# A two-layer graph network on one Trainium2 core: the first pair's transpose moved to TensorE, and the closing work of the last pairs and the planner's VectorE room rearranged

## The chip, the cores and the metric

The kernel runs on one core of a Trainium2 chip. The metric is the device time of one execution in microseconds. Before the change the median of three runs is 1908.55 us (1906.41 to 1909.11); the profiled execution has a span of 1906.8 us. The engines are TensorE (PE in the profile; its weight loads, PEld, are counted apart), VectorE (DVE), ScalarE (ACT), GpSimd (POOL) and SyncE (SP), which issues the transfers. All arithmetic is in float32.

## What is computed

There are 64 graphs of 256 nodes with 512 features, an adjacency of 256 x 256 for each, and two layers. The mask is all ones here.

```python
# layer 0
deg = sum(adj, -1)
agg = (adj @ x) / max(deg, 1e-6)
x   = layernorm(x + relu(concat([x, agg]) @ W.T))
# layer 1
q, k = split(x @ Wqk);  v = x @ Wv
agg  = adj @ (k * mask)
w    = mask * sum(q * agg, -1) / sqrt(512)
x    = layernorm(x + softmax(w, over nodes)[:, :, None] * v)
```

## The kernel before

**Tiling.** Graphs are worked in 32 pairs (`NP`); `k` is the graph of the pair, `t` one of two blocks of 128 nodes, `F` is 512 and `HF` is 256. The products with the weights are done by a Strassen-Winograd scheme of seven products instead of eight, twice nested in part: sums and differences of the blocks of one operand are built first. For the transposed features these are called `xT_s`, `xT_i` (first layer) and `x1T_s`, `x1T_i` (second layer), for the adjacency `sa`, for the aggregated value `tv` (four of them, T1 to T4, made by `sums_T`, line 387). A matrix product with 256 output columns takes two TensorE records, and so does one with 512.

**What a pair goes through.** Layer 0: products with `W` into `own` and `y`; then `gather` (line 401) multiplies the adjacency with `y` and its `tv`, adds parts to `own` and leaves the rest in `z` (this is z's aggregation); `norm0` (line 521) adds `z`, the relu and the residual and normalises `own`, which is then x1. x1 must be transposed for layer 1: `turn` lets VectorE transpose blocks of 32 x 32, and `place` sends the tile `turn` by 16 transfers of 64 KB to `x1T`. Layer 1: products with the weights into `q` (in the tile `y`) and `v`, a second `gather` into `agg`, scores by `dot`. The scores go through DRAM to a row (`send_scores`, `fetch_scores`); `softmax` (line 583) takes the exponentials, `finish` (line 601) adds the weighted `v` to x1 (the steps "adds"), normalises (the steps "finish": `less` on VectorE, two squares and the factor on ScalarE, `shift` on VectorE, two scales on ScalarE) and sends the result out. In the last pair there is no later pair to hide behind, so its x1 is transposed by TensorE (`turn_last`, line 619), into PSUM banks from which ScalarE copies.

**The loop.** Each turn `j` of the loop (line 751) runs layer 0 of pair `j` with layer 1 of pair `j - 1` and the softmax and closing norm of pair `j - 2`. The tail behind the loop (from line 898) does layer 1 of the last pair, the softmax and closing norm of the pair next to last, and then those of the last.

**What sets the order.** Every instruction keeps its place in the program, so the order on each engine is the order of the source's calls. TensorE's order is written out by hand in strings: `run("s s j s a b j", ...)` pops one unit of work from each named list. For the parts that matter here: `r` is the last inner product of layer 0 (which completes `y`), `s` the products whose result goes to the second half of `own`, `a` to `g` are the seven parts of the aggregation (a and b read `y`; c, d, e need `tv` T1, T2, T3; d, e and g write the same PSUM bank as a, so each must wait until the earlier value was read), `j` and `k` are the units of layer 1's first two inner products, `h`, `n`, `q`, `p`, `l` its others.

**The planner.** VectorE's and ScalarE's work that isn't tied to a matrix product stands in chains. A chain has a rank, a name and steps, each for one engine. After each unit `tick` (line 150) takes the first step, in order of rank, whose engine is planned to be free within `room` (0.6 us) of the clock that `mm` advances, and whose `ready` time has come; `step` (line 142) sets this time after a change of engine: 1.4 us after a VectorE step, 2.2 in the closing norms, 0.4 after a ScalarE step. `quiet` stops this, `flush` places all remaining steps of the named chains at once. If VectorE's `tv` are to be spread, `gather` places them one at a time by `spare()`.

Of the kernel before, what the change touches and what calls it, by code (L numbers as in the profile page):

```python
# [94 lines left out]
def resnorm_kernel(  # L95
# [15 lines left out]
    NT, NF, NA = N // P, F // P, A // P  # L111
    H, HF = NF // 2, F // 2
    NP = B // 2
# [16 lines left out]
    clock, chains, shared, quiet = [0.0], [], [1.0], [False]  # L130
    vec = InOrder(tc, nc.vector, clock, lambda name, n: shared[0] * ((0.17 if name == "bn_stats" else 0.07) + n / 960))
    act = InOrder(tc, nc.scalar, clock,
                  lambda name, n: 0.07 + n / 1200 if name == "copy" else (0.3 if n == F else 0.2) + n / 1000)
    gp = InOrder(tc, nc.gpsimd, clock, lambda name, n: 0.0)
    room = {vec: 0.6, act: 0.6}

    def queue(rank, name, *steps, ready=0.0):

        chains.append((rank, name, [ready], deque(steps)))
        chains.sort(key=lambda c: c[0])  # L140

    def step(chain):
        _, name, ready, steps = chain
        eng, work = steps.popleft()
        work()
        ready[0] = eng.free + (2.2 if name == "finish" and eng is vec else 1.4 if eng is vec else 0.4) if steps and steps[0][0] is not eng else 0.0
        if not steps:
            chains.remove(chain)

# [9 lines left out]
    def flush(*names):  # L159
        while True:  # L160
            c = next((c for c in chains if not names or c[1] in names), None)
            if not c:
                return
            step(c)

    def run(order, **units):
        for name in order.split():
            units[name].pop(0)()
# [124 lines left out]
    def inner_sums(X, eng, part):  # L293

        if X.s is None:
            X.open_sums()
        of_sum = lambda n: lambda k, e: X.s[:, k, X.slot[n]:X.slot[n] + 1, e]
        ks, b = ((slice(0, 2), X.first_row), (slice(2, 3), of_sum(S1)), (slice(0, 1), of_sum(S4)))[part]
        a11, a12, a21, a22 = (b(k, e) for k in range(2) for e in range(2))
        i = [X.i[:, r, ks] for r in range(4)]  # L300
        for to, op, c, d in ((i[0], OP.add, a21, a22), (i[1], OP.subtract, i[0], a11),
                             (i[2], OP.subtract, a11, a21), (i[3], OP.subtract, a12, i[1])):
            eng.tensor_tensor(to, c, d, op=op)
# [217 lines left out]
    def norm0(j):  # L521

        own, z, rdeg = owns[j], zs.pop(j), rdegs.pop(j)
        x1Ts[j] = Side(pool, "x1T", S2)
        sq = []

        def scaled(k, t):
            o = own[:, k, t, HF:]  # L530
            vec.scalar_tensor_tensor(o, z[:, k, t], rdeg[:, k, t:t + 1], o, op0=OP.mult, op1=OP.add)

        def residual(k, t, total):
            o = own[:, k, t]
            vec.scalar_tensor_tensor(o, o, 0.0, xs[j][:, k, t], op0=OP.max, op1=OP.add,
                                     accum_out=total[:, t:t + 1])

        def turn(k, t):
            if not sq:
                sq.append(pool.tile([P, 2 * NT * F], F32, name="turn").rearrange(  # L540
                    "p (b k c t q) -> p b k c t q", b=P // Q, k=2, c=NF, t=NT))
            vec.transpose(sq[0][:, :, k, :, t].rearrange("p b c q -> p c b q"), own[:, k, t])

        def place(r):
            to = x1Ts[j].a.rearrange("f k h e t (a q) -> f (k h e t) a q", q=Q)
            for n in r:
                a, b = n // (P // Q), n % (P // Q)
                send(to[b * Q:(b + 1) * Q, :, a],
                     sq[0][a * Q:(a + 1) * Q, b].rearrange("p k c t q -> p (k c t) q"))
        places[0] = place  # L550
        for k in range(2):
            total = small.tile([P, NT], F32, name="sum")
            work = []
            for t in range(NT):
                work += [(vec, lambda k=k, t=t: scaled(k, t)),
                         (vec, lambda k=k, t=t, total=total: residual(k, t, total))]
            steps = work + norm_of(own[:, k], total)
            if j < NP - 1:
                def last(k=k, scale=steps[-1][1]):
                    scale()  # L560
                    queue(1.5, "norm", *[(vec, lambda k=k, t=t: turn(k, t)) for t in range(NT)], ready=act.free + 0.4)
                steps[-1] = (act, last)
            queue(1, "norm", *steps)
# [37 lines left out]
    def finish(j):  # L601

        v, x1 = vs[j], owns.pop(j)

        sums = [small.tile([P, NT], F32, name="sum") for _ in range(2)]

        def add(k, t):
            vec.scalar_tensor_tensor(x1[:, k, t], v[k][:, t], probs[j][:, k, t:t + 1], x1[:, k, t],
                                     op0=OP.mult, op1=OP.add, accum_out=sums[k][:, t:t + 1])

        def last(k, scale):
            scale()
            first(out[2 * j + k].rearrange("(t p) f -> p t f", p=P), x1[:, k])
        queue(0, "adds", *[(vec, lambda k=k, t=t: add(k, t)) for k in range(2) for t in range(NT)])
        for k in range(2):
            steps = norm_of(x1[:, k], sums[k])
            queue(3, "finish", *steps[:-1], (act, lambda k=k, scale=steps[-1][1]: last(k, scale)))

    def turn_last(X, x1, k, ps):
        for t in range(NT):  # L620
            for c in range(NF):
                tc.keep_in_program_order(nc.tensor.matmul(
                    ps[t][:, c * P:(c + 1) * P], x1[:, k, t, c * P:(c + 1) * P], ident, is_transpose=True,
                    start=(c == 0), stop=True, skip_group_check=True))
            act.copy(X.a[:, k, :, :, t].rearrange("p h e m -> p (h e) m"), ps[t].rearrange("p (c m) -> p c m", c=NF))
# [125 lines left out]
    for j in range(NP):  # L751
        X = Xs.pop(j)
# [49 lines left out]
        flush("w0")  # L802
        run("r q r m", m=m, q=q, r=r)
        if j == 1:
            flush("norm")
            places[0](range(16))
            flush("mask")
            sumsM[0] = adj_sums(0)
            load_rows(2)
        quiet[0] = j < 2  # L810
        run("r s r", r=r, s=s)
        if j > 0:
            Y = x1Ts.pop(j - 1)
            inner_sums(Y, gp, 0)
            sums_Y = (*outer_sums(Y, vec), (vec, lambda: inner_sums(Y, gp, 1)))
        if j > 1:
            queue(1, "sums", *sums_Y)
        T_late = []
        T = sums_T(ys[j], T_late)

        if j == 0:
            degrees(1)
# [11 lines left out]
        if j == 0:  # L834
            sums_next()
            held = [c for c in chains if c[1] == "w1"]
            chains[:] = [c for c in chains if c[1] != "w1"]
            early.append(inner("P1", Xs[1], W0, pw[0], u, lambda fifth: early[1](fifth)))
            run("s s a b s d c e i g f", s=s, i=early[0], **g)
            quiet[0] = False  # L840
        else:
            u2, o2, y2 = o, pf, y
            b1, b2, b3, b4, b5, b6, b7, b8 = layer1(j - 1, ys[j][:, :, 0], o2, u2, y2)
            jj = inner("P1", Y, W1, pw[0], u2)
            k = inner("P2", Y, W1, y[0], o2, b2)
            if j == 1:
                run("s s a b s d c e g f", s=s, **g)
                quiet[0] = False
                flush("w1")
                queue(1, "sums", *sums_Y)  # L850
                run("j k j k j k j", j=jj, k=k)
                b1(None)
                run("k", k=k)
            else:
                run("s s j s a b j", s=s, j=jj, k=k, **g)
                if j < NP - 1:
                    degrees(j + 1)
                run("c d j k e j", s=s, j=jj, k=k, **g)
                quiet[0] = True
                run("k", k=k)  # L860
                quiet[0] = False
                b1(None)
                run("g f", **g)
# [34 lines left out]
    send_scores(j - 1)  # L898
    run("l", l=open1)
    flush("norm", "mask")  # L900
    turn_last(X, x1, 0, pf)
    T = sums_T(x1)
    fetch_scores(j - 1)
    sumsM[j] = adj_sums(j)
    turn_last(X, x1, 1, pw)
    inner_sums(X, gp, 0)
    u, o, y = pf, pu, py
    aggs[j] = late.tile([P, 2 * N_SIDE], F32, name="agg").rearrange("p (k t f) -> p k t f", k=2, t=NT)
# [14 lines left out]
    inner_sums(X, gp, 1)  # L923
    run("c d i m e i m", i=i, m=m, **g)
    softmax(j - 1)
    run("g i f i", i=i, **g)
    v = pool.tile([P, 2, NT, F], F32, name="x")
    vs[j] = [v[:, k] for k in range(2)]
    run("m n h h m n h h", h=h, m=m, n=n)
    fourth_sums(X)  # L930
    run("n q q q q n", q=q, n=n)
    flush("softmax", "adds")
    closing = [c for c in chains if c[1] == "finish"]
    for n in (1, 3):
        for c in closing:
            for _ in range(n):
                step(c)
    quiet[0] = True
    run("p p p", p=p)
    for c in closing:  # L940
        step(c)
    run("r p r", p=p, r=r)
    w = small.tile([P, 2, NT], F32, name="w", bufs=1)
    scale_scores(j, w)
    last = [softmax_last(k, w, pu[k]) for k in range(2)]
# [55 lines left out]
```

## Time and profile before

| view | what it shows |
|---|---|
| page, busy times | TensorE 1870.5 us of 1906.8, VectorE 1531.5, ScalarE 1296.3, GpSimd 902.1 |
| windows of 58 us in the middle of the run | TensorE busy 57.6 to 57.9, clock 1.00 |
| window 0 to 100 us | TensorE busy 89.27, mean clock 0.97 |
| window 1856 to 1906 us | TensorE busy 32.48 of 50, mean clock 0.83 |
| groups, VectorE | `turn<-own` x124, 686 ns each; `tv<-y` x64, 721 ns; `x1T_s<-x1T` x64, 693 ns |
| groups, TensorE | transposes at L622 x16, 272 ns a record |
| transfers | `x1T<-turn` x496 of 64 KB, 2.3 us to landing |

The page gives shares over the whole span. The windows say where these shares are not kept: the loop's turns are all alike, the first 100 us and the tail differ. The records of matrix products overlap, so the time that one takes is read from the start of one to the start of the next, not from its length. A bracket at the end of a timeline line gives the idle time of that engine just before it, and what ended it. The helpers at lines 90, 173 and 178 issue nearly everything, so instructions are told apart by the tiles they write and read (`out<-in`).

### The profile page before, as it was taken

How to read it: one execution, taken by the hardware profiler on the slowest of the kernel's cores; microseconds unless marked ns; L12 is line 12 of the kernel's file. 1: busy time of each engine (PE TensorE's matmuls, PEld its weight loads, DVE VectorE, ACT ScalarE, POOL GpSimd, SP SyncE). 2: the span in 40 equal slices, each digit the busy share in tenths (PEclk: the TensorE clock that was granted, in tenths of full speed). 3: DMA queues.
4: the chain of work that ended last, by engine and by line, in shares of the span. 5: the costliest groups of instructions: out<-in, count | busy, mean ns of one | idle time of the engine just before them, and what ended most of it. 6: DMA issues, size and time to landing. Idle time of an engine off the chain costs nothing.

```text
span 1906.8 us, 24867 instructions
## 1 busy us (share of the span) xinstructions
PE 1870.5 (98%) x6980; PEld 1313.5 (69%) x6980; DVE 1531.5 (80%) x3186; ACT 1296.3 (68%) x3266; POOL 902.1 (47%) x1187
## 2 busy tenths in 40 slices
PE   9899999999999999999999999999999999999996
PEld 5567777667677667677677676677776776776774
DVE  7777888878887878887888887888788788878786
ACT  3467776677767677767677766677776777676765
POOL 4455443545444544534554435554445454445431
PEclk9999999999999999999999999999999999999998
DMA  6323334333333433343433343333343333334211
GB/s 222 78 48 96 102 95 112 89 84 98 101 102 94 106 80 99 89 117 84 106 85 98 94 117 84 92 92 106 95 109 91 84 98 98 105 94 107 78 56 45
DMA packets 389160, 182.30 MB, mean 96 GB/s; under 512 B 272160, under 2 KB 353696, under 8 KB 389024
## 3 DMA queue, kind: packets, MB, share of 16 engines
q1 hardware_dynamic: 389024, 180.72, 35.6%
q8 instruction: 57, 0.93, 0.2%
q14 instruction: 79, 0.65, 0.1%
HBM read 114.10 MB, written 34.06 MB: 78 GB/s over the span
## 4 chain that ended last, share of the span: by engine, by line
PE 75%; DVE 12%; SPq 6%; DMA 3%; issue 2%; ACT 1%; POOL 0%; DVEq 0%; POOLq 0%; ACTq 0%
PE bank L173 75%; SPq L178 6%; DVE own L90 4%; DVE y L90 2%; DMA x<-x 2%; DVE x1T_s L90 2%; DVE v L90 1%; DMA x1T<-turn 1%; DVE tv L90 1%; DVE turn L90 1%; ACT y L90 1%; DVE less L90 1%; ACT junk L90 0%; ACT own L90 0%; DVE x L90 0%
## 5 line engine op out<-in xcount | busy, mean ns | idle before, releaser
L90 ACT COPY bank<-bank 128x256 f32<-128x256 f32 (+1 forms) x768 | 332.9, 436 | 196.5 <-PE bank L173 191.0
L90 DVE TENSOR_TENSOR y<-bank,y 128x512 f32<-128x512 f32 x256 | 170.3, 685 | 141.4 <-ACT y L90 137.8
L90 POOL TENSOR_TENSOR x1T_s<-x1T,x1T_s 128x512 f32<-128x512 f32 x32 | 53.1, 1658 | 383.0 <-PE bank L173 383.0
L90 ACT ACTIVATE junk<-own,less 128x512 bf16<-128x512 f32 x252 | 181.6, 721 | 70.3 <-DVE less L90 68.3
L173 PE MATMUL bank<-tv,sa 128*128 128x256 f32 x768 | 199.1, 383 | 5.9 <-DVE tv L90 5.2
L90 ACT ACTIVATE own<-own,shift,rstd 128x512 f32<-128x512 f32 x255 | 197.4, 811 | 0.0
L173 PEld LDWEIGHTS bank<-tv,sa 128*128 128x128 f32 x768 | 142.9, 190 | 64.2 <-issue 22.9
L90 ACT COPY y<-bank 128x512 f32<-128x512 f32 x192 | 108.9, 585 | 96.2 <-PE bank L173 93.4
L90 POOL TENSOR_TENSOR sa<-adj 128x256 f32<-128x256 f32 x128 | 95.5, 746 | 160.9 <-DMA adj<-adj_t 152.2
L173 PE MATMUL bank<-w,x1T_s 128*128 128x512 f32 (+1 forms) x384 | 168.8, 522 | 0.0
L90 POOL TENSOR_TENSOR x1T_i<-x1T 128x256 f32<-128x256 f32 x64 | 57.9, 905 | 234.1 <-DMA x1T<-turn 221.4
L173 PE MATMUL bank<-t_i,x1T_i 128*128 128x256 f32 x512 | 154.1, 384 | 9.8 <-POOL x1T_i L90 5.1
L173 PE MATMUL bank<-t,xT_s 128*128 128x512 f32 (+1 forms) x384 | 159.9, 525 | 0.8 <-ACT own L90 0.3
L173 PE MATMUL bank<-t,x1T_s 128*128 128x512 f32 (+1 forms) x384 | 158.1, 521 | 0.3 <-ACT y L90 0.3
L90 DVE TENSOR_TENSOR v<-bank,v 128x512 f32<-128x512 f32 x186 | 119.1, 681 | 48.9 <-PE bank L173 48.9
L173 PE MATMUL bank<-w,xT_s 128*128 128x512 f32 (+1 forms) x384 | 153.1, 521 | 0.0
L173 PE MATMUL bank<-t_i,xT_i 128*128 128x256 f32 x512 | 152.6, 380 | 0.4 <-DVE own L90 0.2
L173 PEld LDWEIGHTS bank<-t_i,x1T_i 128*128 128x128 f32 x512 | 98.0, 192 | 77.8 <-issue 53.6
L90 ACT COPY own<-bank 128x512 f32<-128x512 f32 x128 | 71.5, 584 | 115.0 <-PE bank L173 74.2
L173 PEld LDWEIGHTS bank<-t_i,xT_i 128*128 128x128 f32 x512 | 94.7, 189 | 58.4 <-issue 46.9
L173 PE MATMUL bank<-t,x1T 128*128 128x512 f32 x256 | 130.4, 592 | 0.0
L90 POOL TENSOR_TENSOR x1T_i<-x1T_s 128x128 f32<-128x128 f32 x128 | 90.2, 705 | 76.3 <-DVE x1T_s L90 73.8
(156 smaller groups left out, 4597.5 us busy)
## 6 DMA issues: line engine op xcount, KB each, us to landing
x<-x SPq DMA_DIRECT2D x64, 512.0 KB, 5.7
xT<-x_t SPq DMA_DIRECT2D x62, 512.0 KB, 5.6
x1T<-turn SPq DMA_DIRECT2D x496, 64.0 KB, 2.3
out<-own SPq DMA_DIRECT2D x62, 512.0 KB, 3.3
adj<-adj_t SPq DMA_DIRECT2D x64, 256.0 KB, 3.8
turn<-adj SPq DMA_DIRECT2D x64, 256.0 KB, 3.0
row<-d SPq DMA_DIRECT2D x31, 256.0 KB, 4.8
wqk<-wqk_t SPq DMA_DIRECT2D x4, 512.0 KB, 5.4
```

The lines of the kernel that those rows point to most:

```text
L90: return self.tc.keep_in_program_order(getattr(self.engine, name)(out, *args, **kwargs))
L173: tc.keep_in_program_order(nc.tensor.matmul(ps, a, b, start=start, stop=True, skip_group_check=True))
L178: return tc.keep_in_program_order(nc.sync.dma_start(out, in_))
```

## The change

It has four edits.

1. **The first pair's x1** is no longer transposed by VectorE and transfers. `turn_last` is now called `turn_here` and is used in the turn `j == 1` too, with `ident` and the two banks `pw`: eight transposes and two copies for each graph. The units of this turn stand in another order, with the first `j` ahead of `g`, and the rest of the second layer's weight sums (`flush("w1")`) ahead of `e`.
2. **The softmax of the pair next to last** is placed as soon as the tail has done `g` and `i`: the exponentials ahead of `f`, and the adds ahead of the work on `v`. The closing norm is left to the planner, where it was placed by hand before the last products.
3. **VectorE is kept free ahead of z's aggregation**: from `j` = 2, its room is -9 from `r s r` until `b`, which keeps the planner from placing anything on it, and the four `tv` are made at once.
4. **The planner's times**: the first step of a closing norm (`less`) is done in the chain "adds", right after the adds of its graph, and opens the chain "finish"; before the two scales of x1's norm the lead after VectorE is 0.7 us instead of 1.4.

```diff
-        ready[0] = eng.free + (2.2 if name == "finish" and eng is vec else 1.4 if eng is vec else 0.4) if ...
+        ready[0] = eng.free + (0.4 if eng is not vec else 2.2 if name == "finish" else 0.7 if len(steps) == NT else 1.4) if ...
...
-            if j < NP - 1:
+            if 0 < j < NP - 1:
                 def last(k=k, scale=steps[-1][1]):
                     scale()
                     queue(1.5, "norm", *[(vec, lambda k=k, t=t: turn(k, t)) for t in range(NT)], ...)
...
-        queue(0, "adds", *[(vec, lambda k=k, t=t: add(k, t)) for k in range(2) for t in range(NT)])
+        work = [[(vec, lambda k=k, t=t: add(k, t)) for t in range(NT)] for k in range(2)]
         for k in range(2):
             steps = norm_of(x1[:, k], sums[k])
-            queue(3, "finish", *steps[:-1], (act, lambda k=k, scale=steps[-1][1]: last(k, scale)))
+            work[k].append((vec, lambda k=k, steps=steps: (steps[0][1](), queue(
+                3, "finish", *steps[1:-1], (act, lambda: last(k, steps[-1][1])), ready=vec.free + 1.4))))
+        queue(0, "adds", *work[0], *work[1])
...
         if j == 1:
-            flush("norm")
-            places[0](range(16))
-            flush("mask")
+            flush("norm", "mask")
...
+        room[vec] = -9.0 if j > 1 else 0.6
         run("r s r", r=r, s=s)
...
-        T = sums_T(ys[j], T_late)
+        T = sums_T(ys[j], T_late if j < 2 else None)
...
             if j == 1:
-                run("s s a b s d c e g f", s=s, **g)
+                turn_here(Y, owns[0], 0, pw)
+                run("s", s=s)
+                turn_here(Y, owns[0], 1, pw)
+                inner_sums(Y, gp, 0)
+                sums_Y = (*outer_sums(Y, vec), (vec, lambda: inner_sums(Y, gp, 1)))
+                run("s b a s d c", s=s, **g)
                 quiet[0] = False
                 flush("w1")
+                run("e j g f", j=jj, **g)
                 queue(1, "sums", *sums_Y)
-                run("j k j k j k j", j=jj, k=k)
+                run("k j k j k j", j=jj, k=k)
...
-                run("s s j s a b j", s=s, j=jj, k=k, **g)
+                run("s s j s a b", s=s, j=jj, k=k, **g)
+                room[vec] = 0.6
+                run("j", j=jj)
...
     softmax(j - 1)
-    run("g i f i", i=i, **g)
+    run("g i", i=i, **g)
+    closing = next(c for c in chains if c[1] == "softmax")
+    while len(closing[3]) > 1:
+        step(closing)
+    run("f i", i=i, **g)
+    flush("softmax", "adds")
...
-    flush("softmax", "adds")
-    closing = [c for c in chains if c[1] == "finish"]
-    for n in (1, 3):
-        for c in closing:
-            for _ in range(n):
-                step(c)
-    quiet[0] = True
-    run("p p p", p=p)
-    for c in closing:
-        step(c)
-    run("r p r", p=p, r=r)
+    run("p p p r p r", p=p, r=r)
```

More of the change, by code (lines that the diff above doesn't have):

```diff
@@ L145, in step @@
         work()
-        ready[0] = eng.free + (2.2 if name == "finish" and eng is vec else 1.4 if eng is vec else 0.4) if steps and steps[0][0] is not eng else 0.0
+        ready[0] = eng.free + (0.4 if eng is not vec else 2.2 if name == "finish" else 0.7 if len(steps) == NT else 1.4) if steps and steps[0][0] is not eng else 0.0
         if not steps:
@@ L613, in last, with turn_here @@
             first(out[2 * j + k].rearrange("(t p) f -> p t f", p=P), x1[:, k])
-        queue(0, "adds", *[(vec, lambda k=k, t=t: add(k, t)) for k in range(2) for t in range(NT)])
+        work = [[(vec, lambda k=k, t=t: add(k, t)) for t in range(NT)] for k in range(2)]
         for k in range(2):
             steps = norm_of(x1[:, k], sums[k])
-            queue(3, "finish", *steps[:-1], (act, lambda k=k, scale=steps[-1][1]: last(k, scale)))
-    def turn_last(X, x1, k, ps):
+            work[k].append((vec, lambda k=k, steps=steps: (steps[0][1](), queue(
+                3, "finish", *steps[1:-1], (act, lambda: last(k, steps[-1][1])), ready=vec.free + 1.4))))
+        queue(0, "adds", *work[0], *work[1])
+    def turn_here(X, x1, k, ps):
         for t in range(NT):
@@ L813, in resnorm_kernel @@
             Y = x1Ts.pop(j - 1)
+        if j > 1:
             inner_sums(Y, gp, 0)
-            sums_Y = (*outer_sums(Y, vec), (vec, lambda: inner_sums(Y, gp, 1)))
-        if j > 1:
-            queue(1, "sums", *sums_Y)
+            queue(1, "sums", *outer_sums(Y, vec), (vec, lambda Y=Y: inner_sums(Y, gp, 1)))
         T_late = []
-        T = sums_T(ys[j], T_late)
+        T = sums_T(ys[j], T_late if j < 2 else None)
         if j == 0:
@@ L900, in resnorm_kernel @@
     flush("norm", "mask")
-    turn_last(X, x1, 0, pf)
+    turn_here(X, x1, 0, pf)
     T = sums_T(x1)
@@ L904, in resnorm_kernel @@
     sumsM[j] = adj_sums(j)
-    turn_last(X, x1, 1, pw)
+    turn_here(X, x1, 1, pw)
     inner_sums(X, gp, 0)
```

## The prediction

> **What bounds the kernel now.** I read the page's busy times and chain first, then the waits of TensorE alone, then TensorE's timeline where it stood still.
>
> ```profile
> PE 1870.5 (98%) x6980; PEld 1313.5 (69%) x6980; DVE 1531.5 (80%) x3186; ACT 1296.3 (68%) x3266; POOL 902.1 (47%) x1187
> PE 75%; DVE 12%; SPq 6%; DMA 3%; issue 2%; ACT 1%; POOL 0%; DVEq 0%; POOLq 0%; ACTq 0%
> ```
>
> TensorE is busy for 98% of the span, and no matmul is removed, so only its idle and slow time can be won. Its waits are short, and two are single events:
>
> ```profile
> PE bank L173 <- ACT bank L90: 6.3, 5, 4.7
> PE bank L173 <- DVE tv L90: 5.2, 17, 1.8
> PE bank L173 <- POOL x1T_i L90: 5.1, 1, 5.1
> ```
>
> (In total, times, longest.) The third line is the first pair's second layer. In the timeline of its stage, the work issued as `j == 1`:
>
> ```profile
> 83.34 1.03 PE L173 MATMUL bank<-y,sa 128*128 128x256 f32 x4
> 89.50 1.22 PE L173 MATMUL bank<-t_i,x1T_i 128*128 128x256 f32 x2 [5.13 <-POOL x1T_i L90]
> 74.66 11.88 SPq L178 DMA_DIRECT2D x1T<-turn  x16
> 88.22 1.23 POOL L90 TENSOR_TENSOR x1T_i<-x1T 128x256 f32<-128x256 f32 x1 [13.52 <-DMA x1T<-turn]
> ```
>
> SyncE issues 16 small transfers for 11.88 us, GpSimd waits for the last landing, TensorE for GpSimd's sums. The longest wait on `ACT bank` is at the end:
>
> ```profile
> 1880.79 1.02 PE L173 MATMUL bank<-t,x1T 128*128 128x512 f32 x2
> 1886.52 1.19 PE L173 MATMUL bank<-t_i,x1T_i 128*128 128x256 f32 x2 [4.71 <-ACT bank L90]
> 1881.76 0.72 ACT L90 ACTIVATE junk<-own,less 128x512 bf16<-128x512 f32 x1 [4.49 <-DVE less L90]
> ```
>
> ScalarE's copy stands behind the squares of the closing norm (`junk`), and these wait for VectorE's `less`. Each gap has a second price in the clock (windows; PEclk is the third from the end):
>
> ```profile
> 89.50:94.10 4.60, 4.60 (x11) 3.50 (x12) 1.63 (x2) 0.71 (x2) 4.50 (x7) 0.50 0.90 301
> 1886.50:1893.20 6.70, 6.15 (x18) 3.82 (x18) 2.06 (x8) 3.21 (x9) 0.00 (x0) 0.52 0.00 0
> ```
>
> The recurring wait, on `tv`, in one stage:
>
> ```profile
> 1474.54 1.03 PE L173 MATMUL bank<-tv,sa 128*128 128x256 f32 x4
> 1475.82 1.13 PE L173 MATMUL bank<-tv,sa 128*128 128x256 f32 x4 [0.26 <-DVE tv L90]
> 1472.96 0.68 DVE L90 TENSOR_TENSOR x1T_s<-x1T 128x512 f32<-128x512 f32 x1
> 1473.68 0.69 DVE L90 TENSOR_TENSOR x1T_s<-x1T_s,x1T 128x512 f32<-128x512 f32 x1
> 1475.07 0.69 DVE L90 TENSOR_TENSOR tv<-y,tv 128x512 f32<-128x512 f32 x1
> ```
>
> Four such records go in 0.86 us elsewhere; here the next four start 1.28 us later, 0.42 us lost, because two `x1T_s` sums (1.4 us) stand ahead of the second `tv`. The same subtraction of starts over the 30 stages from `j` = 2 gives 10.8 us (0 to 0.55 a stage).
>
> **What the Trainium skill says.** "TensorE: Matmul & The Clock Gate", Part 1 (The HAM clock gate): after an idle window of about 3.4 us the array's clock falls to half until a busy window has passed. The trace agrees: gaps of 5.13 and 4.71 us are followed by 0.50 and 0.52, and the 0.25 to 0.7 us waits leave it at 1.00. Its Part 4 (PE-mode transpose): a TensorE transpose lands in PSUM and needs a copy, about 275 ns each in one kernel. Here the records show 272 ns, but overlapped: the 16 at L622 take 1.74 us from first start to the next matmul. "Perfetto Trace Analysis" (Tensor Engine Instruction) says that VectorE's and ScalarE's queues are strictly in order; the tail above shows it.
>
> **Part 1: the first pair's transpose.** Removed: four VectorE transposes (2 x 1.29 us), 16 transfers. Added: 16 TensorE transposes, 1.74 us, all on the path, and four ScalarE copies of 0.51 us (2.05 us for the four at the end). What they read is ready: the first half's scale ends at 67.0, the second's at 72.7; TensorE gets there at 74.1. By the changed order: transposes to 74.9; s to 75.8; transposes to 76.7; s, b, a, s to 80.1, where in the old order b and a follow earlier. Then d accumulates onto a's bank and waits for VectorE, which has b's two operations (0.87), `tv` (0.7) and a's two (0.87) after b ends at 78.4: about 81.0, a new wait of 0.9. d, c, e end at 83.6. GpSimd can start at 77.7, when the copies are out, and its four sums took 4.2 us at 88.22, so by 82 they are there: the first j unit needs no wait and fills the place ahead of g, where TensorE lost 0.9 us to `z`. j, g and f end at 86.2. Before, this same work ends at 91.2, and half speed runs on to 94.1, 1.45 us more. Gain 6.4 us; I take 6.3. Ends: 7.9 (5.3 gap and 2.6 of half speed) less 1.74 with no new wait is 6.1, plus the 1.3 that c and g lost is 7.4; another 1.5 us of copies in line is 5.
>
> **Part 2: the tail.** The softmax exponentials go onto ScalarE at 1864.7, before the y copies (before: 1868.5, after f and i); `adds` follow the fifth-part additions on VectorE, which end at 1866.8: reciprocal, product, four adds of 0.75 to 0.93 and two `less` reach 1870.5. There VectorE sat idle for 3.54 us until 1870.3, so y starts 0.2 late and nothing waits. Squares and factors (4 x 0.81 + 4 x 0.25 = 4.2 us) go between ScalarE's copies from 1870, where it idled 0.22, 1.36, 1.20, 1.13 and 4.49 us. So p and r run on at full clock from 1877.35: six units, then r2, its copy, r3 at 1883.5. VectorE's four x additions (2.5 us) and two dots (1.4) now end at 1882.6, `w` at 1883.0, so the four small transposes run at 1883.5 and their maxima start at about 1884.4; before 1890.76. What follows, ten us of VectorE work and the landing, stays. Gain 6.4 us. Ends: 7.5 (4.7 and all of the clock, 0.43 for each of six half-speed matmuls); 3.5 if two squares (1.6) and 1.3 of copies come in front of what TensorE needs.
>
> **Part 3: every stage from j = 2.** The four `tv` now stand together, then a's and b's additions, then `less` and the `x1T_s` sums; one `less` has moved up between the adds, where VectorE idled 0.55 us. Without `less` x2 (0.66 to the next start), y starts at 1469.6, not 1470.24; y, y, y+fifth and four `tv` end at about 1474.3, a's two operations at 1475.15. TensorE wants d at 1475.40: no wait, 0.25 to spare. Behind the moved work: `x1T_s` is done at 1478.3 instead of 1477.7, its first two at 1477.6 instead of 1474.3; h reads them at 1483.3. GpSimd ends its sums at 1479.8, for n after 1485. Both hidden, in VectorE's 1.77 us of idling for `z` and GpSimd's idling (383 us in all for `x1T_s`). The new order on ScalarE puts one square of the second graph (0.81) behind the last z copy in the place of a degree sum (0.5), so k's copy ends at 1481.75 for a need at 1482.0. The shorter 0.7 lead puts the norm's scale one copy earlier; today's 0.25 us wait there stays or grows 0.1. I take 0.33 won and 0.05 lost a stage: 0.28 x 30 = 8.5 us; ends 10.8 and 0.
>
> **Sum.** 6.3 + 6.4 + 8.5 = 21.2; 1908.55 - 21.2 = 1887.4 us.
>
> **Rivals.** (A) The `tv` wait is only exchanged: a's bank must be read before d, and a's additions now stand behind all four `tv`. Were VectorE 0.4 us later than worked out, d would wait as long as today. For it: 0.25 us is thin, and a `tv` row's longest is 1.65 us. Against: y demonstrably has 0.66 us to come forward. Part 3 gives nothing: 1895.9. (B) One of the ends keeps half of its gap (ScalarE's squares in front of the tail's copies, or copies of x1T late): 3.2 less, 1890.6. For it: VectorE and ScalarE stand in line and one late operation delays all; against: idle time adds up to 8.4 us in the tail. (C) Slower: the second graph's square stands in front of a copy that TensorE waits for in all stages, 0.81 x 30 = 24.3 against 12.7 won at the ends and nothing in part 3: 1920. For it: ScalarE is strictly in order and k's copy has 0.25 us to spare; against: TensorE waited 6.3 us in all for ScalarE's copies, five times, and at 68% ScalarE has room.
>
> **Numbers.** Forecast 0.62, A 0.20, B 0.13, C 0.05. The range goes from 1882.5 (all of part 3 and part 1's upper end: 10.8 + 7.4 + 6.4 is 24.6, and a little in the tail) to A's 1895.9 and 0.6 over it. Under 1904.7 counts as faster: forecast, A and B but for a small rest, 0.94; within 0.02; slower 0.04.
>
> **What would show it.** Right: no TensorE wait over 1 us for GpSimd or ScalarE, clock 1.00 from about 20 us to the end of the tail, 32 transposes, waits on `tv` near zero from j = 2, d in the first stage waiting some 0.9 us for VectorE's `own`. Wrong: waits on `own` of 0.3 us or more in each stage (A), on `bank` or `y` from ScalarE with `junk` ahead of them (C), or a gap over 3.4 us left in the tail (B).

## The result, and the profile after

The kernel after takes 1886.28 us (median of 4 runs, 1884.61 to 1888.67), beside 1907.48 us for the kernel before (4 runs): a ratio of 0.9889, 95% interval 0.9872 to 0.9906. The forecast was 1887.4 us.

The page's busy times and chain of the kernel after:

```profile
PE 1861.3 (99%) x6996; PEld 1312.9 (70%) x6996; DVE 1541.9 (82%) x3182; ACT 1303.6 (69%) x3270; POOL 896.5 (48%) x1187
PE 92%; DVE 5%; ACT 1%; POOL 1%; issue 1%; DMA 0%; DVEq 0%; ACTq 0%
```

TensorE executes more records (the 16 transposes) and is busy for less time; in the two ends no record runs at half clock any more. SyncE and the transfers, 9% of the chain before, are gone from it. TensorE's longest waits (total, times, longest):

```profile
PE bank L173 <- DVE tv L90: 1.8, 1, 1.8
PE bank L173 <- ACT bank L90: 1.6, 4, 0.7
PE bank L173 <- POOL xT_s L90: 1.5, 9, 0.2
PE bank L173 <- DVE own L90: 1.1, 1, 1.1
```

The waits of 5.13 and 4.71 us are gone; of seventeen on `tv`, one is left, in the first stages. New is the third row, nine short waits of the products that read `xT_s`. The row names GpSimd's sum, which was the last to report; but the sum stands at the same point of the stage in e3 below, where nothing waits. What comes later than there, by 0.3 us in the mean of 28 stages, is ScalarE's copy out of these products' bank. The timeline of the first pair's stage, on three engines:

```profile
73.67 1.04 PE L625 MATMUL bank<-ident,own 128*128 128x128 f32 x8
75.40 1.04 PE L625 MATMUL bank<-ident,own 128*128 128x128 f32 x8
81.03 2.94 PE L173 MATMUL bank<-tv,sa 128*128 128x256 f32 x12 [1.15 <-DVE own L90]
83.81 0.59 PE L173 MATMUL bank<-t_i,x1T_i 128*128 128x256 f32 x2
78.92 0.72 POOL L90 TENSOR_TENSOR x1T_i<-x1T,x1T_i 128x256 f32<-128x256 f32 x1
78.99 1.20 DVE L90 TENSOR_TENSOR tv<-y,tv 128x512 f32<-128x512 f32 x1
```

The second `tv` takes 1.20 us beside GpSimd's sum; elsewhere it takes 0.69. The tail and the clock in both ends (windows; PEclk is the third number from the end):

```profile
1867.69 0.67 PE L173 MATMUL bank<-w,x1T_i 128*128 128x256 f32 x2 [0.54 <-ACT bank L90]
81.03:86.50 5.47, 5.47 (x25) 4.53 (x26) 2.86 (x6) 1.53 (x3) 0.00 (x0) 1.00 0.00 0
1867.60:1874.90 7.30, 3.51 (x20) 2.66 (x20) 5.31 (x16) 3.54 (x9) 0.00 (x0) 1.00 0.19 73
```

**Where the 22.3 us of span went**, by matching records of the two timelines: the first `h` product of the first pair's second layer starts at 92.51 instead of 98.71 us; 0.5 of this was there before the stage, so the first pair gives 5.7. The first `own,adj` product of the last pair starts at 1839.58 instead of 1854.66: 8.9 in the stages between. From there to the end it takes 44.96 instead of 52.17: 7.2 in the tail. The forecast was 6.3, 8.5 and 6.4 (the prediction's 0.28 x 30 for the stages is in fact 8.4). The profile of before is a long case of its first pair: from the last `w,xT_i` record ahead of the transposes' place (at 73.95) to that `h` it takes 24.76 us there, 22.9 to 24.7 in the other four kernels below that leave this pair as it was, and 19.06 or 19.07 in all that change it. So one pair of profiles settles the first pair's gain only to within 3.8 to 5.7 us.

**A ledger of the stages.** For the 28 stages between 200 and 1798 us I sum by how much each TensorE record starts later than at full rate after the one before it (0.2135 us for a record of 256 columns, 0.427 for 512, as in undisturbed rows of records; only losses over 0.1 us count), and sort by the operand that the late product needs. This is the second table of the experiments below. From before to after: `tv` 10.3 to 3.5 us, `xT_i` 6.7 to 3.4, `xT_s` **3.0 to 5.5**. The sum, 7.5 us, is most of the 8.9; but the third number goes the wrong way, and for the second the prediction expected no change or a small loss. So part 3 was tested piece by piece.

### The profile page after: what moved, and what is told of

Same layout as the page of the kernel before. It is cut to its first block, busy times and chain, and to the rows that moved or that the text cites. A ratio compares the mean times of both kernels' runs of the same rounds, so it can differ in the third digit from the quotient of the medians.

```text
span 1884.5 us, 24896 instructions
## 1 busy us (share of the span) xinstructions
PE 1861.3 (99%) x6996; PEld 1312.9 (70%) x6996; DVE 1541.9 (82%) x3182; ACT 1303.6 (69%) x3270; POOL 896.5 (48%) x1187
## 4 chain that ended last, share of the span: by engine, by line
PE 92%; DVE 5%; ACT 1%; POOL 1%; issue 1%; DMA 0%; DVEq 0%; ACTq 0%
PE bank L173 92%; DVE own L90 2%; DVE tv L90 1%; DVE y L90 1%; POOL xT_s L90 1%; ACT y L90 0%; ACT own L90 0%; DMA wqk<-wqk_t 0%; PE bank L625 0%; ACT bank L90 0%; DVE st L90 0%; DVE t L90 0%; DVE x L90 0%; DVE v L90 0%; ACT junk L90 0%
## 5 line engine op out<-in xcount | busy, mean ns | idle before, releaser
L173 PE MATMUL bank<-tv,sa 128*128 128x256 f32 x768 | 194.7, 381 | 4.0 <-DVE tv L90 1.8
L173 PEld LDWEIGHTS bank<-tv,sa 128*128 128x128 f32 x768 | 144.8, 190 | 56.0 <-issue 22.9
L90 POOL TENSOR_TENSOR x1T_i<-x1T_s 128x128 f32<-128x128 f32 x128 | 76.6, 598 | 177.4 <-DVE x1T_s L90 174.9
```

What stands on the lines that cost most here:

```text
L90: return self.tc.keep_in_program_order(getattr(self.engine, name)(out, *args, **kwargs))
L173: tc.keep_in_program_order(nc.tensor.matmul(ps, a, b, start=start, stop=True, skip_group_check=True))
```

## The experiments

Twelve kernels ran, each beside the kernel before on the same chip.

| run | what it is | median us | ratio, 95% interval |
|---|---|---|---|
| after | the change | 1886.28 | 0.9889 (0.9872 to 0.9906) |
| e1 | before + edit 1 | 1902.24 | 0.9964 (0.9951 to 0.9976) |
| e2 | before + edit 2 | 1900.82 | 0.9959 (0.9946 to 0.9973) |
| e3 | after, without edit 3 (the hold) | 1885.96 | 0.9879 (0.9865 to 0.9892) |
| e4 | after, lead of 1.4 again | 1888.74 | 0.9893 (0.9880 to 0.9907) |
| e5 | before + idle TensorE filled | 1905.01 | 0.9987 (0.9981 to 0.9994) |
| e6 | before + edit 3 alone | 1915.93 | 1.0047 (1.0035 to 1.0060) |
| e7 | after, `less` back in its chain | 1903.64 | 0.9981 (0.9972 to 0.9989) |
| e8 | after, `tv` spread under the hold | 1900.59 | 0.9964 (0.9952 to 0.9977) |
| e9 | e8, adj loaded ahead of out | 1883.73 | 0.9874 (0.9860 to 0.9887) |
| e10 | e6, adj loaded ahead of out | 1901.84 | 0.9968 (0.9956 to 0.9981) |
| e11 | before + `less` in "adds" alone | 1899.51 | 0.9956 (0.9942 to 0.9970) |
| e12 | e9, closing norm free of the hold | 1876.90 | 0.9836 (0.9822 to 0.9849) |

The ledger (us lost in 28 stages), and three means over these stages: when SyncE issues the load of `adj` and when GpSimd's first `sa` starts, both counted from the stage's first product of `xT_i`, and the time of one `v<-v,fifth` on VectorE. The column `tv` holds the products of `tv` with `sa`; in e6 to e10 a product of `tv` with `adj` loses 1.1 us more, in one stage of the 28.

| run | `tv` | `xT_i` | `xT_s` | `x1T_i` | adj issued | `sa` starts | `v<-v,fifth` |
|---|---|---|---|---|---|---|---|
| before | 10.3 | 6.7 | 3.0 | 0 | -2.63 | 1.92 | 0.59 |
| after | 3.5 | 3.4 | 5.5 | 0 | -2.63 | 1.84 | 0.59 |
| e3 | 7.5 | 3.4 | 0 | 0 | -5.36 | -1.69 | 0.43 |
| e4 | 5.1 | 6.9 | 2.1 | 0 | -2.63 | 1.88 | 0.58 |
| e6 | 4.4 | 6.7 | 10.2 | 3.9 | -1.09 | 3.57 | 0.75 |
| e7 | 3.8 | 3.3 | 11.7 | 4.0 | -1.09 | 3.49 | 0.71 |
| e8 | 0 | 3.4 | 12.3 | 3.8 | -1.09 | 3.57 | 0.72 |
| e9 | 0 | 3.4 | 0 | 4.0 | -5.56 | -1.91 | 0.43 |
| e10 | 1.8 | 6.9 | 0 | 4.1 | -5.57 | -1.90 | 0.43 |
| e11 | 6.4 | 6.9 | 0 | 0 | -5.36 | -1.69 | 0.43 |
| e12 | 0 | 3.4 | 0 | 0 | -5.35 | -1.60 | 0.43 |

### The two ends, each alone (e1, e2), and the price of the clock (e5)

e1 has the transposes on TensorE (the function still under its old name, `turn_last`) and the new order of the turn `j == 1`; e2 has the tail's edit. Of e1:

```diff
-            if j < NP - 1:
+            if 0 < j < NP - 1:
...
+                turn_last(Y, owns[0], 0, pw)
+                run("s", s=s)
+                turn_last(Y, owns[0], 1, pw)
```

> The kernel before with the first edit alone (first pair's x1 transposed by TensorE, units of that turn in the new order). The theory that the three gains simply add: 5.7 us less than before (ratio 0.9970), all of it ahead of 100 us; no half clock there, one wait of about 1.1 us for VectorE's own. Rival, that this edit also frees the transfer queue for what follows (16 transfers of the first pair gone) and so helps the later stages: more than 7 us less, with later stages shorter than before. Rival, that it only pays together with the other edits: under 3 us.

> The kernel before with the second edit alone (softmax and adds of the pair next to last placed sooner, its closing norm left to the planner). Theory that the gains add: 7.4 us less than before (0.9961), all after the last pair's transposes; no gap over 1 us on TensorE in the tail and the clock at 1.00 until the last matmuls. Rival, that the tail needs the first closing step inside the adds chain (here it is in the closing chain of lowest rank): the squares come late, ScalarE's copy waits again, 3 us or less.

Of 1908.99 us, the ratios are worth 6.9 us (4.6 to 9.4) and 7.8 us (5.2 to 10.3). Both ends pay alone, so e2's rival is out. The interval of e1 alone would not exclude its rival of over 7 us, a help to the later stages; but in the ledger these lose 19.1 us in e1 and 19.9 before, so about 1 us at most went that way. With the 8.4 us of e11 below, the parts add up to 23; the change without its third edit (e3) gains 23, the whole change 21 to 22, all within the intervals.

e5 leaves the transfers where they were and fills the idle time in front of the first pair's second layer with four products whose output is written over afterwards:

```diff
                 quiet[0] = False
+                for n in range(4):
+                    tc.keep_in_program_order(nc.tensor.matmul(
+                        pw[0], ident, w0[:, n], start=True, stop=True, skip_group_check=True))
                 flush("w1")
```

> The kernel before with four extra matmuls of 512 columns (3.4 us, into a bank that is free and then overwritten) in the first pair's gap, before the first j unit; nothing else is changed and nothing waits for them. Theory that the clock has a price of its own: it stays at 1.00, the twelve matmul units behind the gap go at full speed, 2 to 2.6 us less than before (0.9987 to 0.9990). Rival, that these units are held by GpSimd's sums anyway (these come one per 1.1 us): the clock stays at 1.00 but the time is the same as before within 1 us. Over 1 us more: the extra matmuls delay the real ones.

The window 80 to 100 us of e5 shows the clock that the kernel before did not have there (0.83):

```profile
80.00:100.00 20.00, 18.30 (x65) 11.54 (x64) 12.80 (x23) 8.69 (x25) 5.87 (x9) 1.00 0.46 112
```

The ratio is worth 2.5 us (1.1 to 3.6). Useless products gain time: from the last `y,sa` record to the first product of `x1T_i` it takes 4.4 us in e5 as in e2 and e6, where nothing fills this time (5.5 in the profile of before), so the wait stayed and the half speed behind it went. The stretch of the first pair that was measured above takes 21.47 us in e5, 24.03 and 23.79 in e2 and e6. The half speed that I read off the windows of before cost 2.6. The two prices of such a gap, the wait and the clock, are separate, and both were real.

### Taking the edits of the stages apart (e3, e4, e6, e7)

e3 takes the hold out of the change (its edit is shown); e6 puts it alone into the kernel before (the same lines the other way round, with the end of the hold after `b`):

```diff
-        room[vec] = -9.0 if j > 1 else 0.6
...
-        T = sums_T(ys[j], T_late if j < 2 else None)
+        T = sums_T(ys[j], T_late)
```

> The changed kernel without the third edit (VectorE's room stays 0.6, the tv are spread as before). Theory that VectorE's hold makes the gain of the recurring stages: the waits of d on tv come back, 7 us more than the changed kernel (0.9927 of before). Rival, that the gain of these stages comes from the shorter lead and the earlier first closing step: within 2 us of the changed kernel (0.989 to 0.990).

Without the hold the kernel is as fast as with it. The waits on `tv` return in part (3.5 to 7.5 us), but those on `xT_s` vanish (5.5 to 0). The rival's outcome came: the hold makes none of the gain.

> The kernel before with the third edit alone (VectorE held free ahead of z's aggregation, the four tv at once). The prediction's step: 8 us less than before (0.9958). Theory of an exchange, after the run in which the hold was taken out of the changed kernel and cost nothing: the waits on tv fall from 10.3 us to under 5, but the work that was held comes late and VectorE reaches the additions for the next turn's products later, so the waits on the banks read by the xT_s products grow by about as much; within 2.5 us of before (0.9987 to 1.0013).

Alone, the hold makes the kernel **slower**, by 9 us (6.7 to 11.4), which neither the prediction's step nor the theory of an exchange had, although it does what it is for: `tv` falls from 10.3 to 4.4. It gives back 7.2 us at `xT_s` and 3.9 at `x1T_i`.

e7 keeps the hold and puts `less` back into the closing norm's chain; e4 puts the lead back to 1.4. The edit of e7:

```diff
-            work[k].append((vec, lambda k=k, steps=steps: (steps[0][1](), queue(
-                3, "finish", *steps[1:-1], (act, lambda: last(k, steps[-1][1])), ready=vec.free + 1.4))))
+            queue(3, "finish", *steps[:-1], (act, lambda k=k, scale=steps[-1][1]: last(k, scale)))
```

> The changed kernel with the first step of the closing norm back in its own chain (no less inside the adds). If the early first step carries the gain of the recurring stages, by bringing y and the squares forward: 3 to 7 us more than the changed kernel (0.9905 to 0.9925 of before). If the shorter lead and the two ends carry it: within 2 us of the changed kernel (0.988 to 0.990).

> The changed kernel with the lead ahead of the two scales of x1's norm at 1.4 us again. By the traces the shorter lead took 3.3 us of waits from the matmuls that read xT_i at the start of each turn and added 2.5 us to those that read xT_s four us later: theory of an exchange, within 1.5 us of the changed kernel (0.989 to 0.990), with the two waits as in the kernel before. Rival, that it is a gain by itself: 3 us slower. The prediction on record had it cost 0 to 0.1 us a stage: then 0 to 3 us faster.

e7 is 17 us slower than the change, far outside both expectations, with about the ledger of e6 at `xT_s` and `x1T_i`. So the step that looked like a detail, one small VectorE operation placed a little earlier, is what pays for the hold. The lead's effect on the time is within the intervals (0.9889 and 0.9893), as the theory of an exchange had it. The ledger shows the exchange: at `xT_i` it divides all kernels alike, 6.7 to 6.9 us with a lead of 1.4 and 3.3 to 3.4 with 0.7; at `xT_s` the change loses 5.5 and e4 2.1, because TensorE comes sooner to a bank that is ready no sooner. Where that bank is ready in time (e3, e9 and e12, against e10 and e11) the lead wins at `xT_i` and `xT_s` stays at 0.

### A first repair that failed (e8)

e8 keeps the hold but lets `gather` spread the `tv`, with c ahead of d in the first turn:

```diff
-        T = sums_T(ys[j], T_late if j < 2 else None)
+        T = sums_T(ys[j], T_late)
...
-                run("s b a s d c", s=s, **g)
+                run("s b a s c d", s=s, **g)
```

> The changed kernel with the tv spread again while VectorE is held (a's additions stand right behind the first tv, so d has both its needs early), and with c ahead of d in the first pair's turn, where d waits 1.15 us. Theory that what is left of the waits of d is only VectorE's order: no wait on tv or own in the recurring stages (3.5 us in the changed kernel), 0.9 us won in the first turn, 3 to 4 us less than the changed kernel (0.9865 to 0.987 of before). Exchange theory: the additions for the next turn still come late, the xT_s waits stay at 5 us or grow, and only the first turn's 0.9 us and some of the 3.5 show: 0.9875 to 0.989.

The waits on `tv` are gone, and the kernel is 14 us slower than the change, outside both expectations: `xT_s` stands at 12.3. In the first turn c ahead of d won nothing either: the stretch measured above takes 19.07 us as in the change, with 0.7 us of waiting for `z` in place of most of that for `own`. Here the trace shows the cause. SyncE, GpSimd, VectorE, ScalarE and TensorE in one stage of e8 (start, length, engine):

```profile
689.25 2.10 SPq L178 DMA_DIRECT2D out<-own  x2
691.47 1.76 SPq L178 DMA_DIRECT2D adj<-adj_t  x2
...
696.47 0.72 POOL L90 TENSOR_TENSOR sa<-adj 128x256 f32<-128x256 f32 x1 [7.37 <-DMA adj<-adj_t]
...
696.59 0.89 DVE L90 TENSOR_TENSOR v<-v,fifth 128x256 f32<-128x256 f32 x1
697.40 0.68 DVE L90 TENSOR_TENSOR v<-bank,v 128x512 f32<-128x512 f32 x1
698.11 0.92 DVE L90 TENSOR_TENSOR v<-v,fifth 128x256 f32<-128x256 f32 x1
...
700.60 1.07 ACT L90 COPY own<-bank 128x512 f32<-128x512 f32 x2 [2.03 <-DVE bank L90]
...
701.33 1.10 PE L173 MATMUL bank<-t,xT_s 128*128 128x512 f32 x2 [0.63 <-ACT own L90]
```

Read upwards: TensorE waits for a bank that ScalarE copies out; ScalarE waited for VectorE's `bank`; VectorE is late because two additions took 0.9 us in place of 0.43; they ran beside GpSimd's `sa`; `sa` had waited for `adj`; and SyncE issues `adj` only behind the results of an earlier pair, `out`. So a transfer that waits for its data holds up those behind it on SyncE, though they need nothing from it. And `out` is late because the closing norm's `shift` is a VectorE step. In all 28 stages of e3 and e11 both shifts run 27.3 us ahead of the next stage's first product of `xT_i`. In e6 to e10, which have the hold and either spread the `tv` or lack the early `less`, both miss this place and run at -9.8, at the turn's end, where `flush("finish")` stands just ahead of the next `load_adj`. In the kernel before, in the change and in e4, one runs at -27 and one at -9.6. The second table says the same of every kernel. Where both transfers of `out` are issued early, or after `adj`, the load of `adj` is issued at -5.4 to -5.6 and `xT_s` costs nothing; where one stands ahead of it, -2.63 and 2 to 5.5 us; where both do, -1.09 and 10 to 12 us. The change with its early `less` only brings one of them forward again.

That VectorE slows down there, and only in some operations, agrees with the Trainium skill, "SBUF — State Buffer" (Who interferes with whom): a VectorE instruction with two inputs in SBUF contends with a GpSimd instruction that reads SBUF; one with at most one such input doesn't, outside the modes that use two ports. `v<-v,fifth` has two, 0.43 alone and 0.89 to 0.92 beside `sa`; `v<-bank,v` has one, the other is in PSUM, and takes 0.68 in the same place as anywhere.

### The transfer's place, tested (e9, e10)

Both kernels only move the issue of `out` behind the load of `adj`; every arithmetic step keeps its place:

```diff
-            first(out[2 * j + k].rearrange("(t p) f -> p t f", p=P), x1[:, k])
+            outs.append((None, lambda: first(out[2 * j + k].rearrange("(t p) f -> p t f", p=P), x1[:, k])))
...
             load_adj(j)
+            run_now(outs)
+            outs.clear()
```

> This is e8 (the change, with the four tv sums spread over the stage under the hold, and c ahead of d in the first turn) with one thing more: the transfers of the finished rows to out are issued right after the next pair's load of adj, where e8 issues them just ahead of it. Theory, the load of adj queued behind out: in e8 both transfers of out came to SyncE late (at 689.25 us in one stage) and the load of adj behind them only at 691.47, some 4.3 us later against TensorE's work than in e3; GpSimd's sums sa ran 5.7 us later, beside VectorE's additions v<-v,fifth, which took 0.89 and 0.92 us in place of 0.42, and the products of xT_s waited 12.3 us and those of x1T_i 3.8 us in 28 stages. With adj ahead of out these waits should fall under 4 us together: 1885 to 1889 us, ratio 0.988 to 0.990, v<-v,fifth at 0.42 us again. Rival, the hold itself makes VectorE's and ScalarE's later work late and the transfer only goes with it: the waits stay near 16 us, 1900 us, ratio 0.996.

> The kernel before with the hold alone, as e6 (1915.9 us, ratio 1.0047), and with the transfers to out issued right after the load of adj. Theory, adj queued behind out: the hold's loss of 14 us in the waits for xT_s and x1T_i (10.2 and 3.9 us in 28 stages) goes, its gain of 6 us in the waits for tv (10.3 to 4.4 us) stays: 1902 to 1904 us, ratio 0.997. Rival, the hold's own lateness: no change against e6, 1916 us, ratio 1.0047.

The first theory holds in both. e9 is 17 us faster than e8, e10 14 us faster than e6, and `xT_s` falls to 0 in each. The transfers of `out` are issued at the same points of the stage as in e8 and e6 (-3.3 and -1.6 us); only `adj` no longer waits behind them. One stage of e9:

```profile
625.43 0.88 SPq L178 DMA_DIRECT2D adj<-adj_t  x2
627.65 2.10 SPq L178 DMA_DIRECT2D out<-own  x2
...
628.91 0.79 POOL L90 TENSOR_TENSOR sa<-adj 128x256 f32<-128x256 f32 x1 [1.42 <-DMA adj<-adj_t]
...
634.99 0.43 DVE L90 TENSOR_TENSOR v<-v,fifth 128x256 f32<-128x256 f32 x1
636.05 0.43 DVE L90 TENSOR_TENSOR v<-v,fifth 128x256 f32<-128x256 f32 x1
...
638.93 1.88 PE L173 MATMUL bank<-t,xT_s 128*128 128x512 f32 x4
```

`adj` is issued ahead of `out`, GpSimd is done with its four sums (at 631.9) before the additions begin, these take 0.43, and TensorE doesn't wait. The one thing in which the expectation was too good: `x1T_i` keeps its 4.0 us in both, so that loss is no child of the transfer. It appears in just the five kernels in which both shifts are late. There six scales of the two norms crowd into the last 8 us of a stage on ScalarE (four or two in the others), as here in e9:

```profile
626.10 2.23 ACT L90 ACTIVATE own<-own,shift,rstd 128x512 f32<-128x512 f32 x3
628.23 0.36 ACT L90 COPY bank<-bank 128x256 f32<-128x256 f32 x1
628.74 0.67 PE L173 MATMUL bank<-t_i,x1T_i 128*128 128x256 f32 x2
```

The copy out of the bank stands behind three scales and ends at 628.59, and the product starts at 628.74, 0.1 us later than at full rate.

### `less` alone, and the version that beats both (e11, e12)

e11 is the kernel before with `less` as the last of the "adds": e7's diff read the other way.

> The kernel before with one half of edit 4 alone: less, the row sums' scaling, taken on VectorE as the last of each graph's additions, the rest of the norm queued from there; lead times as before. Theory, that half is the main part of the gain in the recurring stages: the norm's scales and so the transfers to out come before the next load of adj and of xT, waits for tv and xT_s fall: e3 gains 8.4 us over the first pair's and the tail's parts together, and the lead (e4 against the change) about 2.5 of it, so 6 us here: 1902.5 us, ratio 0.9968. Rival, the gain needs the shorter lead as well: ratio 0.9995 to 1.0, 1908 us.

It gains 8.4 us (5.7 to 11.1), more than expected and as much as the whole recurring part of the change: both `out` are early, `xT_s` goes from 3.0 to 0, and `tv` from 10.3 to 6.4. It needs neither the hold nor the lead. The loss at `xT_s` goes with the earlier `adj`; how much of the fall at `tv` comes from that too, and how much from the room on VectorE that the prediction booked for `less`, no run separates.

e12 adds to e9 that the closing norm isn't held:

```diff
-                if c[2][0] <= clock[0] and c[3][0][0].free <= clock[0] + room[c[3][0][0]]:
+                if c[2][0] <= clock[0] and c[3][0][0].free <= clock[0] + (0.6 if c[1] == "finish" else room[c[3][0][0]]):
```

> e9 (1883.7 us, ratio 0.9874) with one thing more: the closing norm's chain keeps VectorE's usual room of 0.6 while all other work on VectorE is held, so its means, variances and shifts are no longer behind the hold, and ScalarE's scales of own come earlier than in e9, where five of six norm scales ran at 623.8 to 629.3 us among the bank copies that free TensorE's banks. Theory, these late scales are what is left of the hold's cost: the 4.0 us that TensorE loses in 28 stages at the products of x1T_i go, the waits for tv stay near zero: 1880 us, ratio 0.9855. Rival, the loss at x1T_i has another cause, or comes back as waits for tv, since the norm's steps then stand ahead of the tv sums: 1884 to 1886 us, ratio 0.9874 to 0.9885.

The loss at `x1T_i` goes to 0 and `tv` stays at 0: 1876.9 us (1876.39 to 1877.59), below every run of the change. Two of the norm's scales now run at 597.42 and 603.89 us in the stage where e9 had none before 623.79, and four are left at its end:

```profile
624.79 1.52 ACT L90 ACTIVATE own<-own,shift,rstd 128x512 f32<-128x512 f32 x2
626.67 0.36 ACT L90 COPY bank<-bank 128x256 f32<-128x256 f32 x1 [0.35 <-PE bank L173]
```

Here the copy waits for TensorE and no longer for a scale. It is 3 us better than forecast: losses between 0.03 and 0.1 us, which the ledger leaves out, fall from 4.3 to 2.2 us, and the single loss of 1.1 us at a product of `tv` with `adj` is gone. The busy times of e12:

```profile
PE 1855.2 (99%) x6996; PEld 1314.7 (70%) x6996; DVE 1529.0 (82%) x3182; ACT 1304.9 (70%) x3270; POOL 917.7 (49%) x1187
```

## Why the prediction was right, and where it was right by luck

- **Part 1, 6.3 us forecast, 5.7 measured** (3.8 to 5.7 by the other profiles, 4.6 to 9.4 by the times of e1). The mechanism held: 16 transposes, no wait for GpSimd (83.81 has none), clock 1.00, f's end at 86.48 where 86.2 was worked out, though TensorE came to the stage 0.5 us sooner than in the profile of before. The term mis-sized is d's new wait: 1.15 us instead of 0.9, or 1.3 from start to start; 0.2 more went inside d, c and e. VectorE's second `tv` was put at 0.7 us and took 1.20, since GpSimd's fourth sum ran beside it; both rows were known, their overlap wasn't looked at.
- **Part 2, 6.4 forecast, 7.2 measured.** The squares run at 1854.77 to 1861.09 between copies, as the steps had it, and the last wait of TensorE is 0.54 us. Counted from the last pair's first `own,adj` product, the maxima start 6.6 us sooner, where 6.4 was worked out. The other 0.6 us lie behind them, where the sentence "What follows ... stays" put nothing: VectorE's next additions start 1.57 us after the maxima instead of 2.13, and before they had waited 0.50 us for a product of TensorE that ran at half clock.
- **The clock.** 2.6 us for the first gap, read from windows, against 2.5 (1.1 to 3.6) in e5.
- **Part 3, 8.5 forecast, 8.9 measured, and the reasons were wrong: the sum is right by luck.** The prediction gave the whole gain to the hold and the four `tv` at once. The `tv` step held in kind: `tv` won 0.24 us a stage (6.8 us in 28) where 0.33 was taken. But e3 gains as much without it. What failed is the sentence "Behind the moved work: ... Both hidden". It listed `x1T_s` and GpSimd's sums, and left out the closing norm's `shift`, and behind `shift` the scale, `out`, and on SyncE's queue `adj`. Between e3 and the change the hold wins 4.0 us at `tv` and loses 5.5 at `xT_s`; without `less` it loses still more (e6, e7). The second failure is how `less` was booked: as 0.66 us of VectorE time for `y`. It also starts the closing norm earlier: in all it is worth 8.4 us alone, 17 under the hold. The third is the lead's sign: "stays or grows 0.1", where the loss at `xT_i` fell by 0.12 us a stage; in the change `xT_s` takes this back (e4). A gain that the hold did not bring was replaced by one of `less` that was not foreseen.
- **Rivals.** A expected d to lose as much as before; the products of `tv` together lose 0.12 us a stage. B and C did not occur: neither end keeps a wait over 1.15 us, and no `junk` stands just ahead of a copy that TensorE waits for. The nearest to a slower outcome was one that no rival named: the hold without `less`.

What stays open: the 3.4 us at `xT_i`, which the lead halves but no run removed; the split of what `less` gains at `tv`; and the 0.5 us by which the first stages already ran earlier.

## What to carry to other kernels

When work is held back to free an engine, follow each held step to its last consumer, through the other engines and through the queue of transfers: here an output that waited for its data blocked the unrelated load behind it. So issue loads that are ready ahead of stores that may wait, and leave out of the hold the chains that end in a transfer (e12). And a forecast that agrees in its sum is tested only when its terms are: a ledger of lost time by operand, before and after, showed in one table what the total hid.

## What was not expected of the hardware

- A VectorE addition with two SBUF operands takes about twice as long beside a GpSimd sum: 0.43 to 0.92 us (128 x 256), 0.69 to 1.20 us (128 x 512), while one with a PSUM operand keeps its 0.68 us.
- A transfer that waits for its data at SyncE delays the issue of the next: `adj` by 2.7 us with one late `out` ahead of it, by 4.3 to 4.5 us with two.
- Four useless products in a TensorE gap made a kernel 2.5 us (1.1 to 3.6) faster: the wait stayed, and the clock behind it was 1.00 instead of 0.50.
